# A fused LoRA and expert-LoRA kernel, two-level Strassen on one core: the one plain product becomes a Strassen product, four sums of W are made by accumulating transfers, and some steps are planned elsewhere

## The chip, the cores and the metric

The kernel runs on one core of a Trainium2 chip. The metric is the device time of one execution, in microseconds (us); lower is better. Before the change, three executions took 521.52, 521.68 and 522.03 us, median 521.68 us.

## What is computed

`x` is 64 sequences of 64 tokens of 1024 features, in float32. Two residual stages follow each other (cut from the reference):

```python
# stage 0: each sequence has its own adapter of rank 16
x = x + einsum('bnr,bor->bno', einsum('bni,bri->bnr', x, B0[ids0]), A0[ids0])
# stage 1: a dense product, and experts' adapters behind a top-2 gate
base   = einsum('btd,od->bto', x, W)
logits = einsum('btd,ed->bte', x, Wr) + 5.0 * one_hot(ids1)[:, None, :]
gates  = scatter(softmax(top2(logits)))            # two of 8 experts for each token
h      = einsum('btd,erd->bter', x, A1)
x      = x + base + 2.0 * einsum('bter,bte,eor->bto', h, gates, B1)
```

The residual and `base` are one product with W + I (1024 by 1024). It is most of the arithmetic.

## The kernel before

**Tiles.** The tokens lie along the free dimension, features on the partitions. A block is 512 tokens (8 blocks, `k`), two blocks are a pair (`s` = 0 to 3). A block's x is two tiles `x_k_0` and `x_k_1` of 128 by 4 by 512. W is 16 quarters of quarters, `w_ij`, 256 KB each; W + I is made by `add_identity` on the four diagonal ones.

**The product.** A pair's product with W + I is an outer Strassen product of seven, numbered 1, 2, 6, 7, 5, 3, 4 in their order (`ORDER`), in Winograd's form. Its operands are quarters of W: A11, A12 and A22 themselves (products 1, 2 and 4), and sums of them made once, by `outer`: product 5 uses `m5` = A21 + A22, product 7 A11 - A21, product 6 and 3 further sums; these write over quarters of W except for `m5`. Each outer product is again a Strassen product of seven (`product`), with four sums of its weights `s_n_5`, `s_n_6`, `s_n_7`, `s_n_3` made by `weights`, on Pool, and four differences of its tokens `ti_n5`, `ti_n6`, `ti_n7`, `ti_n4` made by `inner_tokens` (on DVE in pair 0). An inner product is four matmuls of 256 columns; each fp32 matmul stands in the profile as two records, so an inner product is "x8". The inner products go to PSUM tiles `pa` (inner 1, 6, 5, 3), `pc` (2) and `pb2` (7, 4), and after each `leave` carries the running sum out, by an ACT copy or a DVE add, to `u`, `v` or an output tile `o`. In the names that the profile shows, buffer numbers are left out: `pb` is pc, pb2 or block k's projection, `s` a weight sum, `w` a quarter, `m` one of `m5`.

The exception is the product named in `WHOLE` (line 254): product 1 of pair 0 is not split. `whole_product` (line 847) does it as four groups of four matmuls with 512 columns (`pw`), each carried to `u` by an ACT copy.

Pair 0's weight sums and quarters are also written to DRAM (`s_kept`), and the later pairs read them back instead of making them again.

**Around the product**, for each block: `turn`, `project` and `adapt` are stage 0 (transposes `pt`, projection `pb` to `bx`, expansion `px`, added to x by DVE); `rows` multiplies x with the experts' A and the router (`ph`, copied to `h` by ACT); `gates` is some twenty small DVE operations for the top-2 softmax, ended by `gated`, which multiplies `h` in place; `weigh` transposes the gated `h` (`pg`, to `hg`), and products with `hg` are added to the inner products of outer 2, 7, 3 and 4. The PSUM tiles `pt`, `px`, `ph`, `pg` and the projection's `pb` share four buffers under the tag `l`.

**The order** is made by a planner (`Plan`, line 34). Each step has an engine with an assumed cost, the tiles it reads and writes, and a due time `at`. `order` sets planned starts, and `issue` writes the steps out in the order of these starts, so each engine's queue has that order. A step's `behind` names data; the step is not planned to start before the steps that make that data have been planned to start. When the program runs, an engine works through its queue in order, and an instruction waits for semaphores only where it needs what another engine or a transfer reads or writes. The SP queue has nearly all transfers; Pool's queue has the gathers of the adapters (`gb`, `ga`) between its sums. The functions `combine`, `outer`, `weights` and, in `products`, `begin` are those around the change.

Of the kernel before, what the change touches and what calls it, by code (L numbers as in the profile page):

```python
# [11 lines left out]
ALU = mybir.AluOpType  # L12
AX = mybir.AxisListType

P = 128
# [18 lines left out]
class Plan:  # L34
# [19 lines left out]
        self.slots, self.shared = slots, shared  # L54
        self.steps = []

    def add(self, eng, fn, reads=(), writes=(), at=0.0, take=(), kb=0, sb=False, behind=()):


        self.steps.append(  # L60
            dict(n=len(self.steps), eng=eng, fn=fn, reads=list(reads), writes=list(writes),
                 at=at, take=list(take), kb=kb, sb=sb, behind=list(behind))
        )

    def order(self):
        steps = self.steps
        wrote, read, users, tag_of, turns = {}, {}, {}, {}, {}
        for st in steps:
            n, dep = st["n"], set()
# [31 lines left out]
        clock, end, where, now = dict(self.SET), {}, {}, {}  # L101
        moved = 0.0
# [28 lines left out]
        while ready:  # L131
            can = {}
            for n in ready:
                for e in steps[n]["eng"]:
                    t = start(n, e)
                    if t is not None:
                        can.setdefault(e, []).append((t, n))
            assert can, [(steps[n]["take"], steps[n]["writes"][:1]) for n in ready]
            e = min(can, key=lambda e: min(can[e]))
            t0 = min(can[e])[0]  # L140
            _, n, t = min((steps[n]["at"], n, t) for t, n in can[e] if t <= t0 + self.LOOK)
            st = steps[n]
            ready.discard(n)
            clock[e] = t + st["eng"][e]
            other = {"DVE": "POOL", "POOL": "DVE"}.get(e)
            if st["sb"] and other in now and clock[other] > t and steps[now[other]]["sb"]:

                mine, theirs = st["eng"][e] / self.PACE[e], (clock[other] - t) / self.PACE[other]
                both = min(mine, theirs)
                clock[e] = t + both + (mine - both) * self.PACE[e]  # L150
                clock[other] = t + both + (theirs - both) * self.PACE[other]
                end[now[other]] = clock[other]
            now[e] = n
            end[n] = clock[e]
            if st["kb"]:
                moved = max(moved, clock[e]) + st["kb"] / self.KB
                end[n] = (moved if e == "SP" else clock[e] + self.GATHER) + self.LAND
            where[n] = e
            st["start"], st["on"] = t, e
            done.append(st)  # L160
            for tag, _ in st["take"]:
                free[tag].remove(min(free[tag]))
                turn[tag] += 1
            for tile_ in held[n]:
                left[tile_] -= 1
                last[tile_] = max(last[tile_], end[n])
                if not left[tile_]:
                    free[tag_of[tile_]].append(last[tile_])
            for m in after[n]:
                needs[m] -= 1  # L170
                if not needs[m]:
                    ready.add(m)
# [9 lines left out]
def kernel(  # L182
# [59 lines left out]
    QC = NC // 4  # L242
    QO = O // 4
# [7 lines left out]
    ORDER = (1, 2, 6, 7, 5, 3, 4)  # L251
    SLOTS = 49

    WHOLE = {(0, 1)}

    pe, dve = Pinned(tc, nc.tensor), Pinned(tc, nc.vector)
    act, pool, sp = Pinned(tc, nc.scalar), Pinned(tc, nc.gpsimd), Pinned(tc, nc.sync)
# [6 lines left out]
    plan = Plan(slots, {"l"})  # L264
# [7 lines left out]
    def new(tag, shape, name):  # L272
        return pools[tag].tile(shape, F32, tag=tag, name=name)
# [33 lines left out]
    bias = const.tile([P, NB * SEQ // P, E], F32, name="bias")  # L307
    dve.tensor_scalar(mask, mask, half, None, ALU.is_equal)
    dve.tensor_copy(order, order_i)
    b1_sb = const.tile([P, O], F32, name="b1_sb")  # L310

# [43 lines left out]
    made = {}  # L355
# [290 lines left out]
    def add_identity(i, at):  # L646
# [10 lines left out]
    quarter = {  # L657
        (i, j): {(k, l): w_name[2 * i + k, 2 * j + l] for k in range(2) for l in range(2)}
        for i in range(2)
        for j in range(2)  # L660
    }
    m_q = {1: quarter[0, 0], 2: quarter[0, 1], 4: quarter[1, 1]}
    s_kept = tc.dram_tile([7, 7, P, QC * QO], F32, name="s_kept")

    def combine(out, a, b, op, at, engines):

        fresh = out not in (a, b)

        def fn(e):
            if fresh:  # L670
                made[out] = new("s", [P, QC, QO], "_".join(str(p) for p in out))
            engine[e].tensor_tensor(made[out], made[a], made[b], op)

        plan.add(engines, fn, [(a,), (b,)], [(out,)], at, [("s", out)] * fresh, sb=True)

    DVE = {"DVE": 0.62}
    POOL = {"POOL": 1.25}

    def outer(n, at):

        if n == 5:
            m_q[5] = {k: ("m5",) + k for k in quarter[1, 0]}
            for k in m_q[5]:
                combine(m_q[5][k], quarter[1, 0][k], quarter[1, 1][k], ALU.add, at, DVE)
        elif n == 7:
            m_q[7] = quarter[1, 0]
            for k in m_q[7]:
                combine(m_q[7][k], quarter[0, 0][k], m_q[7][k], ALU.subtract, at, DVE)
        elif n == 6:
            m_q[6] = quarter[0, 0]  # L690
            for k in m_q[6]:
                combine(m_q[6][k], m_q[5][k], m_q[6][k], ALU.subtract, at, DVE)
        elif n == 3:
            m_q[3] = quarter[0, 1]
            for k in m_q[3]:
                combine(m_q[3][k], m_q[3][k], m_q[6][k], ALU.subtract, at, DVE)
# [3 lines left out]
    def weights(s, n, at):  # L700

        out = {}
        if s > 0:
            for i, m in enumerate(ORDER):
                out[m] = t = ("s", s, n, m)

                def fn(e, t=t, m=m):
                    made[t] = new("s", [P, QC, QO], f"s_{s}_{n}{m}")
                    sp.dma_start(made[t].rearrange("p c o -> p (c o)"), s_kept[n - 1, m - 1])

                plan.add({"SP": 0.1}, fn, [("kept", n, m)], [(t,)], at + i - 8, [("s", t)], kb=256)
            wt[n] = out
            return
        m = m_q[n]
        out = {1: m[0, 0], 2: m[0, 1], 4: m[1, 1]}
        for k, (u, v, op) in {
            5: ((1, 0), (1, 1), ALU.add),
            6: (5, (0, 0), ALU.subtract),
            7: ((0, 0), (1, 0), ALU.subtract),
            3: ((0, 1), 6, ALU.subtract),  # L720
        }.items():
            out[k] = ("s", s, n, k)
            uu = m[u] if isinstance(u, tuple) else out[u]
            vv = m[v] if isinstance(v, tuple) else out[v]
            combine(out[k], uu, vv, op, at - 4, POOL)
        for k in ORDER:
            t = out[k]

            def keep(e, t=t, k=k):
                sp.dma_start(s_kept[n - 1, k - 1], made[t].rearrange("p c o -> p (c o)"))  # L730

            plan.add({"SP": 0.1}, keep, [(t,)], [("kept", n, k)], at + 4, kb=256)
        wt[n] = out
# [51 lines left out]
    def gate_diff(s, at):  # L785
        ha, hb, h = ("hg", 2 * s), ("hg", 2 * s + 1), ("he", s)

        def fn(e):
            made[h] = new("hg", [P, TB], f"he_{s}")
            dve.tensor_tensor(made[h], made[ha], made[hb], ALU.subtract)  # L790

        plan.add(DVE, fn, [(ha,), (hb,)], [(h,)], at, [("hg", h)], sb=True)
# [24 lines left out]
    def products(s):  # L817
        ka, kb = 2 * s, 2 * s + 1
# [9 lines left out]
        def at():  # L828
            return s * SLOTS + slot[0]
# [146 lines left out]
        def begin(n):  # L976
            dest.setdefault(n, n)
            if s == 0 and n in (6, 3):
                outer(n, at() - 4)
            weights(s, n, at() + (6 if (s, n) in WHOLE else 0))  # L980
            if s == 0 and n == 2:
                outer(5, at() + 4)
                outer(7, at() + 8)
            if (s, n) in WHOLE:
                whole_h[n] = {2: ("hg", ka), 3: ("hg", kb), 7: ("hg", kb), 4: ("he", s)}.get(n)
                if n == 4:
                    gate_diff(s, at() - 2)
                return
            inner_tokens(s, n, tokens[n], at())
            if n == 4:  # L990
                gate_diff(s, at() - 2)
            if n in (2, 7, 3, 4):
                gate_sum(s, n, hd, at() - 2)
# [21 lines left out]

        whole_h = {}
        begin(ORDER[0])
        rest = []
        for n in ORDER:
            after = ORDER[ORDER.index(n) + 1] if n != ORDER[-1] else None  # L1020
            if (s, n) in WHOLE:
                for k in rest:
# [110 lines left out]
```

## Time and profile before

| | |
|---|---|
| median of three executions | 521.68 us |
| the profiled execution, its device time | 521.59 us |
| its span, first to last instruction | 519.8 us |
| PE (matmul) busy | 504.9 us, 3432 records |
| DVE busy | 300.9 us, 572 instructions |
| Pool busy | 170.0 us, 141 instructions |
| ACT busy | 41.1 us, 81 instructions |
| moved by DMA | 99.19 MB, of it 8.39 MB by Pool's own queue |
| the four `pw` groups of the whole product | from 28.18 to 43.41 us, with 1.10 us of `px` between |

The profile is of one execution. It has the busy time of each engine, the span in 40 slices of 13 us, the chain of work that ended last (followed back from the last instruction to what released each step), the groups of instructions by operation and tile, and a timeline. All of the kernel's own instructions stand under line 29, the helper that records them, so tiles are what tells them apart. Times below are from the start of the span. The profiled execution's time is 1.8 us more than its span; its time and the median differ by 0.09 us.

### The profile page before, as it was taken

The numbers are of one execution on the slowest core, as the hardware profiler recorded it, in microseconds if no ns is written. First come the engines' busy times: TensorE is split into PE (matmuls) and PEld (weight loads), VectorE is DVE, ScalarE is ACT, GpSimd is POOL, SyncE is SP. The second block draws the span as 40 slices with busy tenths as digits, with TensorE's granted clock in tenths as the row PEclk, the third lists the DMA queues.
The fourth block names the chain that finished last, engine by engine and source line by source line (L and its number), as shares of the span: only waits on it lengthen the run. The fifth ranks groups of instructions, "written<-read, shape, count | busy, mean of one in ns | idle before, by whom it ended". The sixth has DMA issues, their size and how long they took to land.

```text
span 519.8 us, 8542 instructions
## 1 busy us (share of the span) xinstructions
PE 504.9 (97%) x3432; PEld 439.3 (85%) x3432; DVE 300.9 (58%) x572; ACT 41.1 (8%) x81; POOL 170.0 (33%) x141
## 2 busy tenths in 40 slices
PE   2999999999999999999999999999999999999996
PEld 2857988888888988898888998889888898888885
DVE  0699998986953383526684256435486418433632
ACT  1111100002000100012000100000200010000000
POOL 4072067170332144124233313312423322433300
PEclk9999999999999999999999999999999999999999
DMA  7999276799566269716565537744546633610122
GB/s 263 370 367 381 103 263 221 276 326 342 194 202 203 63 194 317 238 61 204 182 224 186 159 101 212 269 149 124 163 161 202 204 95 107 204 62 0 56 104 83
DMA packets 54247, 99.19 MB, mean 191 GB/s; under 512 B 4928, under 2 KB 11072, under 8 KB 54208
## 3 DMA queue, kind: packets, MB, share of 16 engines
q1 hardware_dynamic: 51904, 90.26, 51.6%
q0 software_dynamic: 2304, 8.39, 4.8%
q8 instruction: 27, 0.44, 0.3%
q14 instruction: 12, 0.10, 0.0%
HBM read 69.01 MB, written 29.62 MB: 190 GB/s over the span
## 4 chain that ended last, share of the span: by engine, by line
PE 96%; DMA 2%; DVE 0%; issue 0%; SPq 0%; POOL 0%
PE pa L29 39%; PE pb L29 38%; PE ph L29 11%; PE px L29 3%; PE pw L29 3%; DMA x<-in_xT 2%; PE pt L29 1%; PE pg L29 1%; DVE o L29 0%; SPq L29 0%; DVE bx L29 0%; POOL x L29 0%
## 5 line engine op out<-in xcount | busy, mean ns | idle before, releaser
L29 PE MATMUL pa<-ti,s 128*128 128x256 f32 x432 | 102.5, 380 | 0.0
L29 PE MATMUL pb<-ti,s 128*128 128x256 f32 x384 | 95.8, 380 | 0.0
L29 PEld LDWEIGHTS pa<-ti,s 128*128 128x128 f32 x432 | 80.8, 190 | 11.2 <-issue 0.2
L29 PEld LDWEIGHTS pb<-ti,s 128*128 128x128 f32 x384 | 72.1, 190 | 10.0
L29 PEld LDWEIGHTS ph<-a_sb,x 128*128 128x128 f32 x512 | 62.6, 190 | 1.5 <-issue 0.4
L29 PE MATMUL ph<-a_sb,x 128*128 128x136 f32 x512 | 63.1, 279 | 0.2 <-issue 0.2
L29 POOL TENSOR_TENSOR ti<-x,ti 128x512 f32<-128x512 f32 x24 | 32.2, 1340 | 78.0 <-PE pb L29 77.1
L29 DVE TENSOR_TENSOR o<-pb,o 128x512 f32<-128x512 f32 x47 | 32.4, 690 | 36.1 <-PE pb L29 21.7
L29 PE MATMUL pa<-x,s 128*128 128x256 f32 x216 | 51.9, 379 | 0.0
L29 POOL TENSOR_TENSOR ti<-t,ti 128x512 f32<-128x512 f32 x18 | 25.7, 1429 | 71.0 <-PE pb L29 61.3
L29 POOL TENSOR_TENSOR ti<-x 128x512 f32<-128x512 f32 x24 | 30.8, 1282 | 55.4 <-PE pb L29 41.8
L29 PEld LDWEIGHTS pa<-x,s 128*128 128x128 f32 x216 | 40.1, 190 | 5.3 <-issue 0.3
L29 DVE TENSOR_TENSOR x<-px,x 128x512 f32<-128x512 f32 x64 | 39.8, 684 | 6.8 <-PE px L29 6.8
L29 PE MATMUL pa<-t,s 128*128 128x256 f32 x168 | 41.0, 380 | 0.0
L29 POOL TENSOR_TENSOR ti<-t 128x512 f32<-128x512 f32 x18 | 24.4, 1358 | 42.9 <-PE pb L29 33.4
L29 PEld LDWEIGHTS pa<-t,s 128*128 128x128 f32 x168 | 31.6, 190 | 4.5 <-issue 0.4
L29 DVE TENSOR_TENSOR o<-pa,u 128x512 f32<-128x512 f32 x32 | 22.0, 688 | 20.8 <-PE pa L29 20.1
L29 DVE TENSOR_TENSOR u<-pb,u 128x512 f32<-128x512 f32 x21 | 14.5, 689 | 25.1 <-ACT u L29 20.7
L29 POOL TENSOR_TENSOR s<-w,w 128x512 f32<-128x512 f32 x12 | 17.0, 1418 | 36.0 <-DVE w L29 36.0
L29 PE MATMUL pb<-hg,b_sb 128*128 128x256 f32 x96 | 28.6, 379 | 0.0
L29 DVE TENSOR_TENSOR o<-pa,v 128x512 f32<-128x512 f32 x15 | 10.3, 690 | 25.9 <-PE pa L29 25.9
L29 DVE TENSOR_TENSOR v<-pa,u 128x512 f32<-128x512 f32 x16 | 11.0, 689 | 22.3 <-PE pa L29 22.1
(113 smaller groups left out, 609.5 us busy)
## 6 DMA issues: line engine op xcount, KB each, us to landing
s<-s_kept SPq DMA_DIRECT2D x147, 256.0 KB
x<-in_xT SPq DMA_DIRECT2D x15, 1024.0 KB
out_T<-o SPq DMA_DIRECT2D x30, 512.0 KB
s_kept<-s SPq DMA_DIRECT2D x28, 256.0 KB
s_kept<-w SPq DMA_DIRECT2D x18, 256.0 KB
w<-in_w SPq DMA_DIRECT2D x16, 256.0 KB
x<-in_xT SPq DMA_DIRECT2D x2, 512.0 KB
out_T<-o SPq DMA_DIRECT2D x4, 256.0 KB
```

What stands on the lines that cost most here:

```text
L29: return self._tc.keep_in_program_order(f(*args, **kwargs))
```

## The change

Product 1 of pair 0 is no longer whole: `WHOLE` is empty, so it is seven inner products with four token differences and four weight sums. The four tiles of A21 + A22 (`m5`), before four DVE additions, are each made by two transfers: SP copies a quarter of A21 into the new tile, and Pool issues a transfer that adds the quarter of A22 to it. The planner gets a term `lag` for the accumulating transfer's landing. The planned start of Pool's weight sums for products 1 and 2 of pair 0 is put `behind` the step that writes `h` of block 0 last, which is `gated`. `outer(5)` is due 4 us earlier.

```diff
-    def add(self, eng, fn, reads=(), writes=(), at=0.0, take=(), kb=0, sb=False, behind=()):
+    def add(self, eng, fn, reads=(), writes=(), at=0.0, take=(), kb=0, sb=False, behind=(), lag=0.0):
...
-                 at=at, take=list(take), kb=kb, sb=sb, behind=list(behind))
+                 at=at, take=list(take), kb=kb, sb=sb, behind=list(behind), lag=lag)
...
-                end[n] = (moved if e == "SP" else clock[e] + self.GATHER) + self.LAND
+                end[n] = (moved if e == "SP" else clock[e] + self.GATHER) + self.LAND + st["lag"]
...
-    WHOLE = {(0, 1)}
+    WHOLE = set()
...
-    def combine(out, a, b, op, at, engines):
+    def combine(out, a, b, op, at, engines, behind=()):
...
-        plan.add(engines, fn, [(a,), (b,)], [(out,)], at, [("s", out)] * fresh, sb=True)
+        plan.add(engines, fn, [(a,), (b,)], [(out,)], at, [("s", out)] * fresh, sb=True, behind=behind)
+
+    def gather_sum(out, a, b, at):
+        def copy(e):
+            made[out] = new("s", [P, QC, QO], "_".join(str(p) for p in out))
+            sp.dma_start(made[out], made[a])
+
+        def add(e):
+            pool.dma_start(made[out], made[b], accum_op=ALU.add)
+
+        plan.add({"SP": 0.4}, copy, [(a,)], [(out,)], at, [("s", out)], kb=256)
+        plan.add({"POOL": 1.0}, add, [(out,), (b,)], [(out,)], at, kb=256, lag=2.0)
...
-                combine(m_q[5][k], quarter[1, 0][k], quarter[1, 1][k], ALU.add, at, DVE)
+                gather_sum(m_q[5][k], quarter[1, 0][k], quarter[1, 1][k], at)
...
-            combine(out[k], uu, vv, op, at - 4, POOL)
+            combine(out[k], uu, vv, op, at - 4, POOL, [(("h", 0), 0)] * (n in (1, 2)))
...
-                outer(5, at() + 4)
+                outer(5, at())
```

## The prediction, made before the changed kernel ran

> **What bounds the kernel now.** I read the page first: engine totals, slices and shares of the chain.
>
> ```profile
> PE 504.9 (97%) x3432; PEld 439.3 (85%) x3432; DVE 300.9 (58%) x572; ACT 41.1 (8%) x81; POOL 170.0 (33%) x141
> ...
> PE   2999999999999999999999999999999999999996
> ...
> PEclk9999999999999999999999999999999999999999
> ...
> PE 96%; DMA 2%; DVE 0%; issue 0%; SPq 0%; POOL 0%
> ```
>
> PE is busy from slice 2 to the end. A microsecond taken off PE is a microsecond gained, and a wait that PE does not have now is added in full, because nothing later has slack to win it back. So the question is what the change does to PE's queue. Comparing the two programs' queues, nothing differs in order after about the first 105 us except Pool's gather for block 4, so I look there alone. The chain of waits over that stretch, in order of time:
>
> ```profile
> 26.29 1.89 PE pb L29 x64
> 28.18 3.63 PE pw L29 x8
> 31.81 1.10 PE px L29 x32
> 32.91 10.50 PE pw L29 x24
> 43.41 1.10 PE px L29 x32
> 44.51 1.92 PE pa L29 x8
> 46.44 0.44 PE pg L29 x4
> 46.87 7.42 PE ph L29 x64
> ```
>
> It is all PE, without a gap. The whole product (pw) fills most of 28 to 43 us. The gates' transpose pg, which needs block 0's gated h, comes only at 46.4 us. The timeline shows how late h is made meanwhile:
>
> ```profile
> 27.98 0.49 DVE L29 TENSOR_TENSOR w<-w,ident 128x128 f32<-128x128 f32 x2
> 28.39 0.28 DVE L29 TENSOR_TENSOR bx<-pb,mask 128x128 f32<-128x128 f32 x1
> 28.56 1.26 POOL L29 TENSOR_TENSOR s<-w,w 128x512 f32<-128x512 f32 x1 [16.37 <-DVE w L29]
> 28.59 1.28 DVE L29 SCALAR_TENSOR_TENSOR l<-s,l 128x32 f32<-128x32 f32 x1
> ...
> 33.60 1.28 DVE L29 TENSOR_SCALAR den<-ex 128x4 f32<-128x4 f32 x1
> ...
> 39.66 0.68 DVE L29 TENSOR_TENSOR h<-h,s 128x512 f32<-128x512 f32 x1
> ...
> 56.09 0.19 DVE L29 SCALAR_TENSOR_TENSOR l<-s,l 128x32 f32<-128x32 f32 x1
> ...
> 57.40 0.16 DVE L29 TENSOR_SCALAR den<-ex 128x4 f32<-128x4 f32 x1
> ...
> 58.73 0.69 DVE L29 TENSOR_TENSOR h<-h,s 128x512 f32<-128x512 f32 x1
> ```
>
> The second half of the gates takes 39.66 - 28.59 = 11.07 us in block 0 and 58.73 - 56.09 = 2.64 us in block 1. The operations are the same. In block 0, Pool's eight weight sums (1.26 to 1.29 us each, back to back from 28.56 to 38.66) run beside them, and about every other small DVE operation lasts as long as a Pool sum. Now this costs nothing: pg has over 5 us to spare.
>
> **The change part by part.**
>
> *PE's work.* Out: 32 records of 512 columns, which start 0.43 us apart in the timeline: 13.76 us. In: 7 inner products of 8 records. Back-to-back rows of 256 columns give 0.2158 us each (28 in 6.04): 56 x 0.2158 = 12.08 us. Saved: 1.7 us. This is the whole gain that is in the change for PE.
>
> *The wait on Pool's sums.* `behind` only moves a planned start. Among the waits of the changed program, Pool's first sum s_1_5 has the loads of w_10 and w_11 and DVE's identity added to w_11, the same as before; none on the gates. In DVE's new queue that identity (x2), then bx, still stands right before the second half of the gates. So Pool starts as soon as the identity is done, as at 28.56, and the 11 us stay.
>
> *DVE ahead of the gates.* Product 1's four token differences come in, and one of product 2's moves away: seven instead of four, starting at 22.70. Four end at 25.32; three more at 0.61 to 0.72 us bring the next operation to about 27.2, where it now starts at 26.75 (it had waited for ACT). The gates, bx, the identity and Pool's sums all shift by 0.45 us. h, now without the four identity additions that stood before it at 38.85, starts at 38.85 + 0.45 = 39.3.
>
> *pg.* It comes much earlier in PE's queue: after inner product 1, px, inner product 2 (both of outer product 1) and outer product 2's first. From 28.11: 8 x 0.2158 = 1.73, px 1.10, 16 x 0.2158 = 3.45: PE is there at 34.4. The px tiles hold all four l buffers by then, so pg waits for the DVE addition that frees the first of them, and that stands right behind h: h at 39.3, the addition 0.61 later, done at 40.6. PE waits from 34.4 to about 40.6: **6.2 us**. Queued behind pg on PE are inner products 6, 7 and 5, and the second px; their weight sums are ready by 33, and they wait all the same. No other engine has work that this brings forward.
>
> *What is late next.* From pg: 0.43, three inner products 5.18, px 1.10, inner product 3 1.73, then ph. DVE's additions of the second px are in time for ph (first strip done 0.5 us after px, while inner product 3 takes 1.7). Block 1's gates: ph, then 12 + 8 + 8 records (2.59 + 1.73 + 1.73 = 6.05 us) before the second pg; the gates after ph take, from ph's end at 54.29 to h's end at 59.42 now, 5.1 us. Slack 0.9. The next chain is DVE's rewriting of W, then Pool's sums for product 6. Now it ends at 72.80 for a PE that asks at 72.85: no slack. DVE has 17 operations from the second h to the last rewritten quarter, 17 x 0.61 = 10.4 us, and Pool 1.27 + 1.6 for two sums: 13.3 us after h. PE has 13.9 us of work after pg (64 records), and pg itself is 0.9 behind h: slack about 1.3 us, cost nothing. If PE had not waited at the first pg, it would still be about even. DVE's extra work here (four token differences and three additions for product 1, less four m5 additions, 3 x 0.69 = 2.1 us) lies within PE's 6 us wait.
>
> *The accumulating transfers.* Four DVE additions (0.68 us each) go. SP issues four 256 KB copies, and Pool four accumulating transfers; the trace has none of the latter. Nearest row: a Pool gather takes 0.94 to 1.11 us to issue, 1.3 us apart, and 7.4 to 8.4 us to land for 512 KB. SP's copies stand behind two s_kept writes that need the identity on w_22 and w_33 (at about 43). Pool's four stand behind the gather that needs the second px: issued from about 50 to 55, landed by 58 to 63. DVE reads the first at about 67 and the last at 73: 10 us of cover, cost 0. Moved past on SP's queue are s_kept writes, which nobody in this stretch reads; on Pool's, the sums for product 6, which wait for DVE until 73 anyway. From below no gain: the DVE time saved lies in PE's wait. From above: landing twice as slow makes the last 5 us late, less 1.3 slack: 4 us. The Trainium skill ("SBUF — State Buffer", "A bandwidth-pool intuition that's wrong") speaks against such transfers: a Pool-queue DMA of 620 ns takes some 3100 ns beside a DVE copy that locks the shared port. The rows here show gathers at 38.81 to 44.89 with DVE busy at 0.94 to 1.08 us, no longer than the 1.11 at 2.88 with DVE idle. By the rows, 4 x 1.3 = 5.2 us; by the rule 12.4, which still lands before 73. I take 0.
>
> *PE's clock after the wait.* Since 13.7 us PE has had no gap over 0.4 us. The nearest row is the start:
>
> ```profile
> 9.72 1.94 PE L29 MATMUL pt<-ident,gb 128*128 128x128 f32 x8 [9.72 <-DMA gb<-in_b,idx]
> ...
> 61.47 1.04 PE L29 MATMUL pt<-ident,gb 128*128 128x128 f32 x8
> ```
>
> After idling, eight transposes take 0.90 us more than later, and the next 32 small projections 1.54 instead of 1.08, 0.46 more: 1.4 us lost, although the granted clock is written as full. The Trainium skill ("TensorE: Matmul & The Clock Gate", "What's actually happening") says that an idle window of some 3.4 us halves PE's clock until PE has been busy for such a window; a wait of 6.2 us is long enough, mostly. By the granted-clock row the cost would be 0; by the start's rows 1.4; by the rule 1.7 (half of 3.4), at most 3.4 if the window falls badly. I take 1.4, the row.
>
> **Sum.** -1.7 + 6.2 + 1.4 = +5.9 us. 521.6 (the profiled execution, 0.1 from the median) gives **527.5 us**.
>
> **The rivals.**
> 1. *Faster:* Pool's sums do start behind the gates, so these take 2.64 us. h starts at 29.04 + 2.64 = 31.7 and the first l buffer is free at 33.0, before PE arrives at 34.4. Pool starts at 31.8 and its second sum, which inner product 6 needs, ends at 34.3, when pg is just running. PE's 1.7 us then stand: 520.0. It decides at h before about 33. For it: block 1's 2.64 us. Against it: the program has no such wait. Chance 0.08.
> 2. *The blocking eases*, because small DVE operations slip between Pool's sums at another phase, and h comes 3 us sooner. The wait is 3.2 us, under the length at which the clock would suffer: 521.6 - 1.7 + 3.2 = 523.1. Against it: the eight sums and the DVE operations start in the same relation as now. Chance 0.06.
> 3. *The accumulating transfers land late*: 527.5 + 4 = 531.5. For it: no row of one. Against it: 10 us of cover. Chance 0.06.
> My forecast has 0.80; its own range is 525.5 (no clock penalty, gates 0.6 early) to 529.5 (penalty 3.4).
>
> The range is 524.8 to 529.8: the forecast with 0.7 us more at the early end and 0.3 at the late end, leaving out the three rivals, 0.20. A measurement of this kernel tells about 0.2% (1 us) from no change. Faster: 0.08, from rival 1. Same: 0.03, half of rival 2's lower half. Slower: 0.89.
>
> **What would show it.** Right: an idle of about 6 us on PE before the first pg, ended by DVE (x<-px); small DVE operations of block 0's gates still over 1 us; Pool's first sum at about 29; PE's next records slower; no other new idle on PE up to 110 us. Wrong: Pool's first sum after 31, with the gates in 3 us; an idle before inner product 6 of product 1 that Pool ended; an idle at about 75 to 80 us ended by Pool or a transfer of m5.

## The result, and the profile after

The changed kernel takes 528.02 us (median of four executions, 527.16 to 529.12) against 521.72 us: ratio 1.0121, 95% interval 1.0109 to 1.0132, 6.3 us slower. The granted clock, averaged over the span, is 0.994 in each of the four, and 0.998 to 1.0 in every execution of the kernel before that has one on record. The profiled execution is the longest of the four: 529.12 us, with a span of 527.3.

The page after: engine totals, PE's slices, the granted clock by slice, and the chain's shares.

```profile
PE 507.0 (96%) x3456; PEld 446.8 (85%) x3456; DVE 303.5 (58%) x575; ACT 41.1 (8%) x81; POOL 174.2 (33%) x145
...
PE   2978999999999999999999999999999999999997
...
PEclk9997999999999999999999999999999999999999
...
PE 93%; DVE 4%; DMA 2%; issue 1%; DVEq 0%
```

Slices 3 and 4 of PE (26 to 53 us) are no longer full. In slice 4 the granted clock is 0.7, and DVE has come into the chain. The loss stands in the chain of waits over that stretch:

```profile
38.24 1.15 DVE s L29
39.41 0.04 DVE h L29
...
41.02 0.69 DVE x L29
41.71 0.04 issue
41.75 1.11 PE pg L29 x4
42.87 3.41 PE pa L29 x8
46.28 2.26 PE pb L29 x8
48.54 1.73 PE pa L29 x8
```

PE's transpose pg starts when DVE's addition x<-px has freed the l buffer, right behind h. The next eight records take 3.41 us and the eight after them 2.26; only the third group is back at 1.73. The timeline of the same stretch shows why h is late:

```profile
29.77 0.49 DVE L29 TENSOR_TENSOR w<-w,ident 128x128 f32<-128x128 f32 x2
...
30.35 1.34 POOL L29 TENSOR_TENSOR s<-w,w 128x512 f32<-128x512 f32 x1 [17.56 <-DVE w L29]
30.38 0.18 DVE L29 SCALAR_TENSOR_TENSOR l<-s,l 128x32 f32<-128x32 f32 x1
...
34.23 1.28 DVE L29 TENSOR_SCALAR den<-ex 128x4 f32<-128x4 f32 x1
34.36 1.89 PE L29 MATMUL pa<-x,w 128*128 128x256 f32 x8
...
39.41 1.69 DVE L29 TENSOR_TENSOR h<-h,s 128x512 f32<-128x512 f32 x1
...
41.75 1.11 PE L29 MATMUL pg<-ident,h 128*128 128x128 f32 x4 [5.51 <-DVE x L29]
...
42.66 3.62 PE L29 MATMUL pa<-ti,s 128*128 128x256 f32 x8
...
46.07 2.47 PE L29 MATMUL pb<-ti,s 128*128 128x256 f32 x8
...
48.38 1.89 PE L29 MATMUL pa<-ti,s 128*128 128x256 f32 x8
```

Pool's first sum starts as soon as DVE has added the identity ("<-DVE w"), not behind the gates. The second half of the gates takes from 30.38 to 39.41, 9.0 us, because small operations such as den<-ex still last as long as a Pool sum. PE, done with its last product at about 36.1 (34.36 and eight records of 0.2158), idles 5.5 us in the profile's count.

The books go from the start of product 1 to the second pg. These rows are before, and then after:

```profile
28.11 3.70 PE L29 MATMUL pw<-x,w 128*128 128x512 f32 x8
...
61.03 0.60 PE L29 MATMUL pg<-ident,h 128*128 128x128 f32 x4
```

```profile
29.50 1.99 PE L29 MATMUL pa<-x,w 128*128 128x256 f32 x8
...
66.59 0.60 PE L29 MATMUL pg<-ident,h 128*128 128x128 f32 x4
```

Before, this is 61.03 - 28.11 = 32.92 us. After, it is 66.59 - 29.50 + 2.59 = 39.68; the 2.59 us are product 2's inner product 7, which the changed kernel has behind that pg. The difference of 6.76 us has three parts:

- the wait from 36.09 to 41.75: 5.66 us;
- slow records: 2.74 us (from start to start, the transpose takes 0.91 us in place of 0.43, inner product 6 3.41 in place of 1.73, inner product 7 2.31 in place of 1.73);
- a saving of 1.64 us, which is what is left over.

This execution is 7.5 us longer than the profiled one of before. Its start gives 1.39 us of that: projection pb of block 1 begins at 27.61 in place of 26.22, and PE's work up to there is not changed. Behind the second pg it wins back 0.6 us in small pieces, whose cause stays open. Without the late start 6.1 us are left, and the medians differ by 6.3.

### The profile page after: what moved, and what is told of

Read it like the earlier page. It is cut to its first block, busy times and chain, and to the rows that moved or that the text cites. A ratio compares the mean times of both kernels' runs of the same rounds, so it can differ in the third digit from the quotient of the medians.

```text
span 527.3 us, 8614 instructions
## 1 busy us (share of the span) xinstructions
PE 507.0 (96%) x3456; PEld 446.8 (85%) x3456; DVE 303.5 (58%) x575; ACT 41.1 (8%) x81; POOL 174.2 (33%) x145
## 4 chain that ended last, share of the span: by engine, by line
PE 93%; DVE 4%; DMA 2%; issue 1%; DVEq 0%
PE pa L29 39%; PE pb L29 38%; PE ph L29 10%; PE px L29 3%; DMA gb<-in_b,idx 1%; PE pt L29 1%; DVE x L29 1%; DVE ti L29 1%; PE pg L29 1%; DVE s L29 1%; DVE w L29 0%; DVE c L29 0%; DMA ids_sb<-in_ids 0%; DVE den L29 0%; DVE d L29 0%
## 5 line engine op out<-in xcount | busy, mean ns | idle before, releaser
L29 PE MATMUL pa<-ti,s 128*128 128x256 f32 x448 | 108.2, 385 | 0.0
L29 PE MATMUL pb<-ti,s 128*128 128x256 f32 x392 | 98.2, 382 | 0.0
L29 PEld LDWEIGHTS pa<-ti,s 128*128 128x128 f32 x448 | 84.9, 193 | 12.0 <-issue 0.4
L29 PEld LDWEIGHTS pb<-ti,s 128*128 128x128 f32 x392 | 74.2, 191 | 10.3
L29 PE MATMUL pa<-x,s 128*128 128x256 f32 x224 | 53.9, 380 | 0.0
L29 POOL TENSOR_TENSOR ti<-x 128x512 f32<-128x512 f32 x24 | 30.5, 1269 | 51.2 <-PE pb L29 36.1
L29 PEld LDWEIGHTS pa<-x,s 128*128 128x128 f32 x224 | 41.6, 190 | 5.4
L29 DVE TENSOR_TENSOR u<-pb,u 128x512 f32<-128x512 f32 x24 | 16.5, 688 | 25.1 <-ACT u L29 20.7
L29 DVE TENSOR_TENSOR o<-pa,v 128x512 f32<-128x512 f32 x15 | 10.3, 690 | 24.4 <-PE pa L29 24.3
```

What stands on the lines that cost most here:

```text
L29: return self._tc.keep_in_program_order(f(*args, **kwargs))
```

## The experiments

Theory A, that of the prediction: Pool's sums block the gates, PE waits for the late h, and its clock falls in the wait. The rivals: B, DVE's added work is what is late wherever PE waits; C, splitting costs the loss; D, the transfers cost it. Each ratio is to the kernel before, run on the same chip (521.67 us for the first four kernels, 522.01 for the others).

**The wait made real** (to the changed kernel):

```diff
+            if out == ("s", 0, 1, 5):
+                pool.tensor_copy(made[out][:, 0, :1], made["h", 0][:, 0, :1])
             engine[e].tensor_tensor(made[out], made[a], made[b], op)
```

> The changed kernel, with the wait made real: ahead of Pool's first sum of W, Pool copies one column of block 0's gated h into that sum's tile, so Pool's sums cannot start before the gates are done. No order of instructions changes otherwise. Theory A (Pool's sums block the small DVE operations, PE waits for the late h, and its clock falls in the wait): the second half of the gates takes about 2.6 us in place of 9, PE finds the first l buffer free when it comes to the gates' transpose, waits at most 0.5 us for Pool's second sum, and the clock stays full: 520.0 to 521.0 us. Rival B (DVE's added work is what is late, and the wait moves on to the next use of DVE's results): the first wait goes, but one of several us comes at the second gates or at product 6's weight sums, 524 to 528 us.

Measured: 520.26 us, ratio 0.9967 (0.9956 to 0.9978). Its timeline:

```profile
29.83 0.18 DVE L29 SCALAR_TENSOR_TENSOR l<-s,l 128x32 f32<-128x32 f32 x1
...
31.13 0.16 DVE L29 TENSOR_SCALAR den<-ex 128x4 f32<-128x4 f32 x1
...
32.38 0.69 DVE L29 TENSOR_TENSOR h<-h,s 128x512 f32<-128x512 f32 x1
...
33.22 0.18 POOL L29 COPY s<-h 128x1 f32<-128x1 f32 x1 [20.96 <-DVE h L29]
33.49 1.27 POOL L29 TENSOR_TENSOR s<-w,w 128x512 f32<-128x512 f32 x1
...
35.53 0.60 PE L29 MATMUL pg<-ident,h 128*128 128x128 f32 x4
```

The second half of the gates takes 2.55 us (29.83 to 32.38) in place of 9.0. Pool's copy waits for h, and pg runs without a wait. After it no matmul waits to the end of the span. One added instruction takes back the 6.3 us and 1.4 more, and this version beats both kernels; its granted clock is 0.998 to 1.0 in all seven executions. Rival B falls: DVE has the same work here.

**The transpose planned later** (to the changed kernel):

```diff
-        weigh(k, at + 6)
+        weigh(k, at + (19 if k == 0 else 6))
```

> The changed kernel, with the transpose of block 0's gated h planned later: on PE it now stands behind ph of block 1, so inner products 6, 7 and 5 of product 1 come ahead of it. Pool's sums and the gates are as late as before. PE then comes to the second px at about 40 us, which needs all four l buffers, freed by DVE up to 43.4 us. Theory A: a wait of 3 to 4 us in place of 5.6, so 2 us less, and of the clock's penalty of about 2.5 us some or all goes[...]: 523.5 to 525.8 us. Theory B (DVE's work is the bound, the place of the wait does not matter): 527 to 528 us.

Measured: 523.93 us, ratio 1.0055 (1.0039 to 1.0072). PE's timeline:

```profile
38.67 1.89 PE L29 MATMUL pa<-ti,s 128*128 128x256 f32 x8
41.10 1.08 PE L29 MATMUL px<-bx,ga 32*128 32x128 f32 x4 [0.54 <-DVE x L29]
...
43.79 1.15 PE L29 MATMUL px<-bx,ga 32*128 32x128 f32 x26 [0.56 <-DVE x L29]
44.88 1.99 PE L29 MATMUL pa<-x,s 128*128 128x256 f32 x8
```

px takes from 40.4 to 44.9 us, 3.4 more than its 1.1, in pieces with idles of at most 0.6 us, and the profiled execution (523.6 us) has no slow records after it. Three executions took 523.6 us, with a granted clock of 0.998 or 0.999; one took 524.2, with 0.996, and two 525.9, with 0.993. So the longer ones ran at a lower clock, though none of them was traced. B would have left 527 or more.

**The wait filled with work** (to the changed kernel; the added products are zero):

```diff
+                if (s, n, k) == (0, 2, 1):
+                    for x in range(12):
+                        pe.matmul(
+                            made[ps][:, x % QC, :], zero, tx()[:, 0],
+                            start=False, stop=True, skip_group_check=True,
+                        )
```

> The changed kernel, with 12 matmuls of zeros (24 records of 256 columns, 5.2 us of PE) added to outer product 2's first inner product, right ahead of the gates' transpose: they fill the wait and add zero to the sum, so only PE's idling goes, and everything that PE waits for comes when it did. Theory A: the clock stays full, and the slow records after the wait (inner product 6 in 3.4 us in place of 1.73, inner product 7 in 2.26, the transpose in 1.1) go back to their pace: 2.4 to 2.9 us less, 525.1 to 525.7 us. If those records are slow for another cause than the idling (their operands, DMA), the time stays at 528 us or rises.

Measured: 525.2 us, ratio 1.0071 (1.0058 to 1.0084). PE's timeline:

```profile
34.77 5.34 PE L29 MATMUL pa<-x,zero 128*128 128x256 f32 x24
40.47 0.66 PE L29 MATMUL pg<-ident,h 128*128 128x128 f32 x4 [0.35 <-DVE x L29]
40.96 1.89 PE L29 MATMUL pa<-ti,s 128*128 128x256 f32 x8
```

pg waits 0.35 us, and inner product 6 runs at full pace (40.96 to 42.69). With the time of the wait still spent, 2.8 us come back (528.02 - 525.2), which is the 2.74 us of slow records in the books. The granted clock is 0.999 or 1.0 in all five executions, where the changed kernel has 0.994. So the idling makes the records slow, not their operands.

**Each part alone.** First the split alone (to the kernel before):

```diff
-    WHOLE = {(0, 1)}
+    WHOLE = set()
```

> The kernel before, with product 1 split and nothing else of the change: A21 + A22 by four DVE additions, and no plan that holds Pool's sums. The planner then puts the gates' transpose behind four more inner products on PE. Theory A: Pool's sums still block the gates, h comes at about 40, but PE reaches the transpose only at about 41; a wait of about 1.4 us at the second px for the l buffers and one of 1.5 us at product 6's first weight sums (DVE has 2.1 us more work and the m5 additions stand ahead of it), 1.7 us saved on PE: 522 to 524 us. Rival C (splitting costs the whole loss): 527 to 528 us.

Measured: 524.95 us, ratio 1.0067 (1.0054 to 1.008). There is loss, but mostly not where it was expected: the second px takes 0.8 us more than its 1.1 (expected 1.4), and product 6 does not wait. PE waits at product 2's inner product 5 for DVE's addition to o, which the four m5 additions (m<-w,w) stand ahead of:

```profile
60.80 1.04 PE L29 MATMUL pt<-ident,gb 128*128 128x128 f32 x8
...
61.27 2.49 DVE L29 TENSOR_TENSOR m<-w,w 128x512 f32<-128x512 f32 x4
...
63.67 0.68 DVE L29 TENSOR_TENSOR o<-pa,u 128x512 f32<-128x512 f32 x1
...
64.41 3.36 PE L29 MATMUL pa<-ti,s 128*128 128x256 f32 x8 [2.57 <-DVE o L29]
...
67.57 2.25 PE L29 MATMUL pa<-t,w 128*128 128x256 f32 x8
...
69.65 1.03 PE L29 MATMUL pa<-x,s 128*128 128x256 f32 x4
```

After a wait of only 2.57 us the records are slow: 64.41 to 67.57 and to 69.65 are 5.24 us for two inner products of 1.73, 1.8 us lost. The granted clock is 0.995 to 0.997 in five of the six executions and 0.999 in the fastest (524.31 us), so the lowering is not the same in each. The wait, the slow records and px, less the saving of 1.64, come to 3.5 us; the split without the transfers costs 3.3 us (524.95 - 521.67), mostly through DVE's queue. That is rival C's direction, at half its size; whether it holds with the transfers is the subject of the experiment without the hold, below.

The hold alone (to the kernel before):

```diff
-            combine(out[k], uu, vv, op, at - 4, POOL)
+            combine(out[k], uu, vv, op, at - 4, POOL, [(("h", 0), 0)] * (n in (1, 2)))
```

> The kernel before with only the planned hold put in: product 1 stays whole and DVE makes the sums. The planner, which takes the hold for real, puts the gates' transpose behind the second of the four 512-column groups. Pool in fact starts at 28.6 as ever. Theory A: PE comes to the transpose at 36.3 us, h and the freed l buffer come at 40.1: a wait of 3.8 us, and 1 to 2.5 us of slow records after it: 525.5 to 528 us. If the hold is harmless without the split: 521.7 us.

Measured: 525.64 us, ratio 1.0077 (1.0064 to 1.0091). From the timeline:

```profile
28.84 0.18 DVE L29 SCALAR_TENSOR_TENSOR l<-s,l 128x32 f32<-128x32 f32 x1
...
33.10 3.70 PE L29 MATMUL pw<-x,w 128*128 128x512 f32 x8
...
36.64 1.69 DVE L29 TENSOR_TENSOR h<-h,s 128x512 f32<-128x512 f32 x1
...
38.99 0.65 PE L29 MATMUL pg<-ident,h 128*128 128x128 f32 x4 [2.19 <-DVE x L29]
39.48 3.60 PE L29 MATMUL pw<-x,w 128*128 128x512 f32 x8
```

The hold moves pg into the whole product, where it waits 2.19 us, less than the 3.8 expected: the second half of the gates took only 7.8 us here (28.84 to 36.64). This execution has no slow records, and it is the fastest of its five (524.03; the others 525.35 to 526.78). Three of the other four have a granted clock of 0.999 or 1.0, so it is not a lower clock that makes them longer; a later h would, but none was traced. The longest has 0.996. The planned hold costs by itself, without the split.

The transfers alone (the kernel before, with `gather_sum` for `combine` in `outer(5)`, due 4 us earlier):

> The kernel before with only the accumulating transfers put in: product 1 stays whole, no hold. DVE loses 2.7 us of additions that PE does not wait for, Pool's queue gains four issues that stand before sums waiting for DVE anyway. Theory A: no difference, 521.2 to 522.2 us. Rival D (the transfers cost): more than 523 us.

Measured: 521.44 us, ratio 0.9992 (0.9985 to 0.9998). As good as nothing: PE has no wait, so D falls.

**Without the hold** (to the changed kernel, the `behind` of `weights` taken out again; split and transfers stay):

> The changed kernel without the planned hold on Pool's sums: product 1 split and the accumulating transfers stay. The planner then puts the gates' transpose behind inner products 6, 7, 5, 3 of product 1 and the first of product 2, as in the split alone. Theory A (the hold does not hold Pool, it only moves the transpose to where h is not yet made): PE reaches the transpose at about 41 us, when h is there; no wait there; and with DVE spared of the four m5 additions the wait of 2.6 us that the split alone had at product 2's inner product 5, with its slow records, goes too: 520.0 to 521.2 us. Rival D (the transfers are what costs): as slow as the split alone or slower, 525 us or more.

Measured: 521.28 us, ratio 0.9985 (0.9978 to 0.9991), a gain of 0.7 us. The row of inner product 5:

```profile
62.61 1.99 PE L29 MATMUL pa<-ti,s 128*128 128x256 f32 x8 [0.36 <-DVE o L29]
```

pg does not wait. px takes 2.0 us in place of 1.1 for its l buffers, and the wait at inner product 5 is 0.36 us in place of 2.57. These two, 1.3 us together, are enough to explain why it falls short of the real wait (ratio 0.9967, which is 0.9 us less). With the transfers the split costs nothing, so C falls as well.

**The real wait with DVE's sums** (the first experiment, with `combine` for `gather_sum`, due as before the change):

> The real wait of the first experiment, with A21 + A22 by DVE additions as before the change in place of the transfers. Theory A with the transfers off DVE's path: the four additions (2.4 us) stand ahead of the addition that frees product 2's accumulator; DVE had 0.4 us to spare there and the second pt moves 0.4 us of PE ahead of it: a wait of about 1.6 us, and some of the clock's loss: 522 to 524 us. If DVE has slack enough, 520.3 us as with the transfers.

Measured: 521.62 us, ratio 0.9995 (0.9987 to 1.0004). The row of inner product 5:

```profile
63.49 1.99 PE L29 MATMUL pa<-ti,s 128*128 128x256 f32 x8 [1.24 <-DVE o L29]
```

PE waits 1.24 us at the place named, and the records after it keep their pace. So the transfers are worth something once PE is no longer held by the gates: the real wait has 0.9967 with them and 0.9995 without.

## Why the prediction was right

It forecast 527.5 us in a range of 524.8 to 529.8; 528.02 was measured. By its steps:

- *PE's work*, 1.7 us saved: 1.64 by the books, as what is left over there. Right.
- *The hold holds nothing*: right. Pool's first sum follows the identity, at 30.35 in an execution that started 1.39 us late, so 28.96 for a forecast of about 29. Making the wait real removes the loss; the hold alone adds one.
- *DVE's shift*, 0.45 us: the gates begin at 28.55, which is 27.16 without the late start, against 26.75 before: 0.41.
- *The wait at pg*, 6.2 us: 5.66 measured. PE arrived 0.3 us later and the l buffer came 0.3 us earlier than worked out. That the sum is so near is in part luck: the gates' second half took 9.0 us in place of the 10.3 worked out (29.04 to 39.3), while h itself was blocked too (1.69 us for 0.68), which the prediction did not have. The second rival, that the blocking eases at another phase, was thus true in a small part.
- *PE's clock*, taken as 1.4 us from the start's rows: 2.74, and 2.8 by the filler. The mechanism was right; this is the mis-sized term. The start's row was a bad measure, because its slow stretch is of no fixed length: the first 64 small projections took 1.54 and 1.08 us in the profile before, and 3.98 in the one after. Both estimates from the rule of the Trainium skill ("TensorE: Matmul & The Clock Gate", "What's actually happening"), 1.7 us and at the widest 3.4, were nearer than the row that I took. But that rule's idle window of some 3.4 us is not the least that slows the records here: 2.57 us of idling did it in the split alone. So the second rival's wait of 3.2 us need not have been free of slow records.
- *The transfers*, cost 0: right. Pool issues them from 54.8 to 58.5 us (forecast from about 50 to 55), 5.1 to 7.0 us pass to landing, and DVE reads them from 70.3 to 76.2 us.
- *DVE's next chain*, about even: right with the transfers. The real wait has no wait there; without the transfers it has 1.24 us, at the addition to o and not at product 6's sums, which the prediction had named as the tight place.
- *The rival that Pool is held*, forecast at 520.0: made real, it measured 520.26.

The two errors, 0.5 us too much in the wait and 1.3 too little in the clock, partly cancel, and the 0.6 us that is won back later was not forecast. The mechanism is shown; that the total came within 0.5 us of the forecast is in part luck.

What stays open: why 2.57 us of idling slowed the records (the split alone) and 2.19 did not (the hold alone, in the execution that was profiled). The program alone does not decide it: one and the same kernel had a granted clock of 0.993 in some executions and 0.999 in others (the transpose planned later), and one of the 21 executions of the transfers alone took 523.5 us at 0.996, where the traced one has no wait. What makes three executions of the hold alone longer at a full clock also stays open.

## What to carry to other kernels

A planner's order is not a wait. When a step is to stay away from another engine's work, look in the program for the semaphore that makes it so; if there is none, the plan is only believed by the steps that it moves, here PE's transpose, moved up to meet an h that was not made. On a saturated engine price such a wait at its length and the slow records behind it: here 5.66 us of waiting cost 8.4. And judge a relief of a second engine by what PE waits for around it: the transfers were worth about 0.4 us where PE had no wait, about 1.5 with the split and the wait made real, and about 4.3 with the split alone (1.0067 without them, 0.9985 with them), where PE waited for an addition that stood behind DVE's sums.

## What the runs showed of the hardware

The granted clock was 0.74 over 39 to 52 us in the profile after, from a single wait of 5.5 us:

```profile
39.00:52.00 13.00, 10.25 (x63) 8.53 (x64) 7.50 (x15) 1.75 (x3) 4.89 (x6) 0.74 1.00 348
```

(The columns are the stretch, its length, the busy time of PE, PE's weight loads, DVE, ACT and Pool, the clock, DMA's share and GB/s.) A wait of 2.57 us lowered it too (the split alone, 0.87 over 65 to 78 us). Its row has the same columns:

```profile
65.00:78.00 13.00, 13.00 (x54) 11.17 (x53) 11.44 (x15) 0.00 (x0) 4.64 (x4) 0.87 0.70 259
```

With the transpose planned later it was 0.993 over the span in two executions of six. Where it fell there was not traced; the traced execution, at 0.999, has no idle over 0.6 us from 20 us on.

Beside Pool's sums, DVE operations of 0.16 us lasted up to 1.3 us. The chain of small operations was held up by a different amount in each trace: the gates' second half took 7.8, 9.0 and 10.2 us in three traces with Pool's sums beside it (the hold alone, the changed kernel, the transpose planned later), and 2.55 us without them. DVE's additions that read PSUM kept their 0.68 us, as here in the real wait:

```profile
37.34 1.33 POOL L29 TENSOR_TENSOR s<-w,s 128x512 f32<-128x512 f32 x1
...
37.46 0.68 DVE L29 TENSOR_TENSOR x<-px,x 128x512 f32<-128x512 f32 x1
```

An accumulating transfer of 256 KB took 0.84 to 1.70 us of Pool to issue and 4.1 to 8.9 us to land, over the kernels that have them.
